# Cross-attention on one Trainium2 core: opening loads on three queues, one context value per slot, and the last values in the score banks

## The chip, the core and the metric

The kernel runs on one core of a Trainium2 chip. The metric is the time of the device in microseconds (us), lower is better. The core has a matrix engine (TensorE, "PE" in the profile, its weight loads "PEld"), three engines for elementwise work (VectorE "DVE", ScalarE "ACT", GpSimd "POOL") and a queue engine that only issues transfers (SyncE, "SP"). ACT and POOL can issue transfers too, from queues of their own. Matrix products are accumulated in PSUM, eight banks of 128 x 512 float32; everything else lies in SBUF, 128 partitions.

## The reference

The input x is 32 batches of 512 rows of 640 columns, the context 32 batches of 77 rows of 1024. The other key and value weights of the signature belong to context rows behind the 77th, which these inputs do not have; only the text part and the outer frame of it count:

```python
q = _heads(hidden_states @ to_q_w)             # 20 heads of 32
k, v = _heads(ehs_txt @ to_k_w), _heads(ehs_txt @ to_v_w)
s = jnp.einsum('bhqd,bhkd->bhqk', q, k) * scale
p = jax.nn.softmax(s, axis=-1)
out = _merge(jnp.einsum('bhqk,bhkd->bhqd', p, v)) @ to_out_w + to_out_b + hidden_states
```

All of it is float32. The kernel keeps this precision by splitting each operand of a large product into a high part (a cast, "hi") and the rest (a subtraction, "lo"), and adding three products: hi x hi, hi x lo, lo x hi.

## The kernel before

The 640 columns are five chunks of 128, each of four heads. A *unit* n is one chunk of one batch, n = 5 b + j; there are 160. The order of the work on every engine and queue is the order in which the program writes it down (a manual schedule); semaphores are put in by the framework. There are four stretches.

*Opening and context, lines 265 to 397.* PE first runs 15 warm-up matmuls on a tile of zeros. The context (2464 rows) is taken in groups of 512 columns, the last of 416, and contracted over eight blocks of 128, k = 0 to 7. For each k three things are loaded, context (cs, line 149), key weights and value weights (wraw, line 99), each as four transfers, one for each quarter of the partitions. VectorE transposes the context (L157), ScalarE casts context and weights (L89), VectorE subtracts (L90), PE forms keys and values (pk and pv, L182). For k = 0 the key products go in three passes: hi x hi for all five chunks, then hi x lo of the context, then lo of the weights. `first` (line 271) writes this down for the first group. Before it stand the first loads: four context quarters on SP, two weight quarters on ACT behind a small copy, two on SP; then POOL waits for the first context quarter (`pause`) and issues the value weights of k = 0 and 1. Keys and values go to DRAM, and are read back per batch (kb and vb). Groups 0 to 3 are done here, and the keys of the last group; its values, five products of 24 matmuls each (`context_values`, chunk by chunk), are left for the next stretch.

*Slots, units 0 to 7, `slot` at line 667.* In slot n PE forms the scores of unit n (L454), the queries of unit n + 1 (L437), and, from slot 3 on, the values of unit n - 3 (L553). VectorE takes maxima (L475), ScalarE takes exponentials (L515) into pn, POOL divides by the sums (L527), VectorE transposes the result into z (`transpose_p`, L534; two buffers, z0 for even units and z1 for odd), and SP moves z into raw with four transfers (`move_p`, L543), which is what PE reads for the values. There are two raw buffers. There is one query buffer (qt0) in this stretch: VectorE copies the queries of unit n + 1 from PSUM into it (L449) before the scores of n + 1. The five values of the last context group are worked in between: chunks 0 and 1 ahead of slot 0, chunk 2 in slot 0, chunks 4 and 3 in slot 1. SP loads the five blocks of output weights (`load_wo`, L665) in slot 1.

PSUM and SBUF change hands in this stretch. Four banks ("sc") hold scores, one ("pq") queries; until the last context value three banks belong to `psv`, after it they become one "po" and two "pa". Where ScalarE has not emptied a score bank in time, `LENT` lets a unit take po or pa for part of its scores. In SBUF the first three value-weight chunks lie in `kva` (wv_s0), the last two with the split context in `kvp` (wv_s1, ct, vs). When these are released the output weights (pool `lw`) take the place of kva, and the pool `late` that of kvp: it holds, in this order, z1 and the two raw buffers, then the rest. In bytes of a partition wv_s0 ends, and wv_s1 begins, at 169952; wv_s1 ends at 186336; z1 takes 168576 to 174720, the first raw buffer 174720 to 182912, the second 182912 to 191104, where ct begins at 186336. The pools are opened with waits per tile: a new tile waits for the last use of those old tiles whose bytes it takes.

*Windows, units 8 to 159, `window` at line 727.* Two units at a time: values, scores of two units, exponentials, one output product (`group`, L602) with its transposition (`turn`, L612) and addition, and queries. Five windows make two batches; the change does not touch them.

*End, `closing` (line 814) and `end` (line 826).* In the last window no queries remain; `closing` puts two output products of the last batch but one in the banks pq and po, turns them, and then takes the values of unit 156 into pq. `end` takes those of 157 into po and the further output products into pq and po again, then the last batch's projection (L634).

Of the kernel before, what the change touches and what calls it, by code (L numbers as in the profile page):

```python
# [37 lines left out]
def kernel(  # L38
# [53 lines left out]
    def load_weights(w, k0, kn, permuted=True, queues=(nc.sync,) * 4, tag="wraw"):  # L92


        raw = kvw.tile([P, 2, C], F32, tag=tag, name="wraw", bufs=3 if tag == "wraw" else 2)
        if permuted:
            rows = w.rearrange("(q c i) n -> q i c n", q=4, i=Q)
            for q, queue in enumerate(queues):
                queue.dma_start(raw[q * Q : (q + 1) * Q, :kn], rows[q, :, k0 : k0 + kn])  # L99
        else:  # L100
            rows = w.rearrange("(c p) n -> p c n", p=P)
            nc.sync.dma_start(raw[:, :kn], rows[:, k0 : k0 + kn])
        for k in range(kn):
            wraws[id(w), k0 + k] = raw[:, k]

    def split_weights(dst, w, k, scale=None, turned=False):

        part = wraws.pop((id(w), k))
        if scale is not None:
            nc.scalar.mul(part, part, scale)  # L110
        hi, lo = dst[:, 0, :], dst[:, 1, :]
        if turned:
            part = part.rearrange("p (q c i) -> p c q i", q=4, i=Q)
            hi, lo = (d.rearrange("p (c q i) -> p c q i", q=4, i=Q) for d in (hi, lo))
        split(hi, lo, part)
# [20 lines left out]
    GROUPS_KV = [(g0, min(G, NT - g0)) for g0 in range(0, NT, G)]  # L136
    cts, pks, pvs, css, craws, wraws = ({} for _ in range(6))

    def load_context(g, *counts):

        g0, gn = GROUPS_KV[g]
        src = ehs_flat[g0 : g0 + gn, :].rearrange("(a j) (q u) -> q j a u", j=Q, q=4)
        if g not in css:
            css[g] = kvc.tile([P, G // Q, NK * Q], F32, tag="cs", name="cs"), [0]
        cs, done = css[g]
        for kn in counts:
            cols = slice(done[0] * Q, (done[0] + kn) * Q)
            for q in range(4):
                nc.sync.dma_start(
                    cs[q * Q : (q + 1) * Q, : gn // Q, cols], src[q, :, :, cols]  # L150
                )
            done[0] += kn
# [9 lines left out]
    def split_context(g, k):  # L162
        gn = GROUPS_KV[g][1]
        ct = kvp.tile([P, 2, G], FPR, tag="ct", name="ct", bufs=9)
        split(ct[:, 0, :gn], ct[:, 1, :gn], craws.pop(k)[:, :gn])
        cts[g, k] = ct
# [57 lines left out]
    def context_values(g, j, pool):  # L224
        values_of(g, j, pool)
        split_values(g, j)
# [44 lines left out]
    def first(*ks):  # L271

        for k in ks:
            transpose_context(0, k)
        for k in ks:
            split_context(0, k)
            split_weights(wk_s[:, k], wk, k)
            for passes in ((0,), (1,), (2,)) if k == 0 else ((0, 1, 2),):
                for j in range(NC_):
                    keys(0, j, k, passes)  # L280
            part = wraws.pop((id(wv), k))
            for (c0, c1), dst in zip(WV, wv_s):
                split(dst[:, k, 0], dst[:, k, 1], part[:, c0:c1])
            for j in range(3):
                values_of_chunk(0, j, k, psk)

    early = kvt.tile([P, P], F32, name="early", bufs=1)
    load_context(0, 1)
    nc.scalar.copy(early[:, :Q], zero[:, :Q].bitcast(F32))
    load_weights(wk, 0, 1, queues=(nc.scalar, nc.scalar, nc.sync, nc.sync))  # L290
    pause = kvt.tile([P, P], F32, name="pause", bufs=1)
    probe = css[0][0][:Q, 0, :Q]
    nc.gpsimd.tensor_tensor(pause[:Q, :Q], probe, probe, ALU.add)
# [237 lines left out]
    def transpose_p(n):  # L531

        pn, z = pnb[n % 2], zs[n % 2]
        nc.vector.transpose(  # L534
            z.rearrange("p c h t j -> p (h t) c j"),
            pn.rearrange("p a (c i) -> p a c i", i=Q),
        )
# [112 lines left out]
        elif h == 1:  # L650
            nc.sync.dma_start(out[last, rows, :], xr)

    LATE, LAG = 2, 3
    EARLY_X = {4: 0, 6: 1}
    LENT = {3: {0: "po", 1: "pa"}, 4: {2: "po", 3: "pa"}, 6: {2: "po", 3: "pa"}}
    held, wos = [], []

    def take(m, tag="pa"):
# [4 lines left out]
    def load_wo(ks):  # L663
        for k in ks:
            nc.sync.dma_start(wos[0][:, k].bitcast(F32), wo_dram[:, k].bitcast(F32))  # L665

    def slot(n, beside=()):
        b, j = divmod(n, NC_)
        copied, last = 3 <= n <= 6, n == FIRST - 1
        views = scores(n)  # L670
        maxima(n, views)
        while held:
            low_a(held.pop())
        if n and not copied and not last:
            transpose_p(n - 1)
        if n == 1:
            load_wo(range(3))
        if j == 0:
            load_keys(b + 1)
        if j == 1:  # L680
            load_values(b)
        if n == 1:
            load_wo(range(3, NC_))
        if n == 0:
            load_x(2)
            load_y(0, range(4))
        for i in range(2):
            exps(n, i)
        if last:
            transpose_p(n - 1)  # L690
        if n >= LATE and not last and not copied:
            move_p(n - 1)
        if len(beside) > 1:
            context_values(LAST, beside[1], psv)
        queries(n + 1, "po" if last else "pq")
        copy_q(n + 1, nc.vector.tensor_copy)
        if copied:
            transpose_p(n - 1)
            move_p(n - 1)
        if n >= LAG and not last:  # L700
            values(n - LAG)
        if last:
            qts.append(late[0].tile([P, S], F32, name="qt1"))
            queries(n + 2)
            copy_q(n + 2, nc.vector.tensor_copy)
        for i in range(2, HPC):
            exps(n, i)
        if not last:
            normalize(n)
        if n == 1:  # L710
            for i in range(NQ):
                transpose_x(2, i)
        if beside:
            context_values(LAST, beside[0], psv)
        if n >= LAG and not last:
            high_a(n - LAG)
            held.append(n - LAG)
        if n in EARLY_X:
            split_x(2, EARLY_X[n])
        if n == 3:  # L720
            load_bias()
        if n < 3:
            split_x(1, n + 2)
# [90 lines left out]
    def closing(n):  # L814

        last = B - 1
        for t in range(NQ):
            load_residual(t)
        for c, tag in ((1, "pq"), (2, "po")):
            group(last - 1, c, range(NC_), tag)  # L820
            turn(last - 1, c)
            add(last - 1, c)
        values(n - 2, "pq")
        high_a(n - 2)

    def end():
# [53 lines left out]
    for c in range(2):  # L880
        split_x(1, c)
    context_values(LAST, 1, psv)
    slot(0, (2,))
    kva.release()
    lw = ctx.enter_context(tc.tile_pool(name="lw", bufs=1, reuse_waits="tile"))
    wos.append(lw.tile([P, NC_, 2, C], FPR, name="wo_s"))
    slot(1, (3, 4))
    psv.release()
    kvp.release()
    late.append(ctx.enter_context(tc.tile_pool(name="late", bufs=1, reuse_waits="tile")))  # L890
# [2 lines left out]
    )  # L893
    zs.append(late[0].tile(ZSHAPE, F32, name="z1"))
    move_p(0)
    for n in range(LATE, FIRST):
        slot(n)
    for n in range(FIRST, N, 2):
# [42 lines left out]
```

## Time and profile before

| what | us |
|---|---|
| median of 3 runs | 1691.91 (1691.86 to 1692.5) |
| profiled execution, its own time | 1692.86 |
| its span, first to last instruction | 1690.8 |
| TensorE busy | 1683.6 |
| ScalarE busy | 1075.9 |
| VectorE busy | 1010.5 |
| GpSimd busy | 990.1 |

The profile is that of one execution. In a timeline a row gives start, duration, engine, line and operation, "out<-in" by tile names, shapes, a count where rows are merged, and in brackets how long the engine had been idle and what released it. "SPq", "ACTq" and "POOLq" are transfers being issued, not moving. In the table by engine a row is a stretch: its length, then the busy time of PE, PEld, DVE, ACT and POOL with the number of instructions, then the granted TensorE clock, the DMA engines' busy share and GB/s. The chain of waits follows back from the last instruction what released each step. A row of transfers gives count, size and the median time from issue to landing.

### The profile page before, as it was taken

The page shows a single profiled execution, that of the slowest core. Times are in us where ns is not written, and L with a number is a line of the kernel's source. Part 1 is how long each engine was busy: PE and PEld are TensorE (multiplying, and loading weights), DVE is VectorE, ACT ScalarE, POOL GpSimd, SP SyncE. Part 2 cuts the span into 40 slices and gives each one's busy share as a digit, 9 for nine tenths or more (in the row PEclk, how much of TensorE's full clock was granted, in tenths as well). Part 3 has the DMA queues.
Part 4 walks back from the last instruction along what each step waited for, and adds up shares of the span by engine and source line. Part 5 has one row for each costly group of instructions (what it writes and reads, how often), then busy time and mean ns, then how long its engine had stood idle before and what let it go on. Part 6 is the DMA issues. An engine that isn't in the chain of part 4 may idle for free.

```text
span 1690.8 us, 36827 instructions
## 1 busy us (share of the span) xinstructions
PE 1683.6 (100%) x12460; PEld 1303.9 (77%) x12460; DVE 1010.5 (60%) x1635; ACT 1075.9 (64%) x5622; POOL 990.1 (59%) x663
## 2 busy tenths in 40 slices
PE   9999999999999999999999999999999999999999
PEld 7888898777777777777777777777777777777777
DVE  4341235766676666766666657576666766667653
ACT  3231125867677676776767767677676776767762
POOL 1000026667667666667575766767667676766755
PEclk9999999999999999999999999999999999999999
DMA  9847558678889787879797988888979788888956
GB/s 182 159 94 189 121 103 229 150 173 188 190 187 204 172 204 175 202 181 212 166 211 166 211 181 195 185 194 186 203 173 204 173 202 190 188 192 183 210 136 187
DMA packets 363852, 306.51 MB, mean 181 GB/s; under 512 B 88784, under 2 KB 292112, under 8 KB 363664
## 3 DMA queue, kind: packets, MB, share of 16 engines
q1 hardware_dynamic: 360864, 296.61, 78.4%
q0 software_dynamic: 2704, 7.38, 1.4%
q8 instruction: 99, 1.62, 0.4%
q14 instruction: 89, 0.73, 0.1%
q10 hardware_dynamic: 96, 0.16, 0.0%
HBM read 120.36 MB, written 57.88 MB: 105 GB/s over the span
## 4 chain that ended last, share of the span: by engine, by line
PE 97%; DMA 1%; ACT 0%; DVE 0%; SPq 0%; issue 0%; POOL 0%; DVEq 0%; ACTq 0%
PE pq L437 32%; PE po L602 31%; PE pv L182 7%; PE pk L182 7%; PE sc L454 6%; PE po L553 4%; PE pq L553 4%; PE pa L454 3%; DMA wraw<-in_L_xattn_to_k_w_dram 1%; PE sc L634 1%; PE pa L553 0%; ACT pn L515 0%; DMA cs<-in_ctx_dram 0%; PE pa L634 0%; PE pq L602 0%; SPq L99 0%
## 5 line engine op out<-in xcount | busy, mean ns | idle before, releaser
L515 ACT ACTIVATE pn<-sc,nm 128x77 f32<-128x77 f32 x1928 | 597.3, 367 | 131.4 <-DVE nm L508 102.8
L437 PE MATMUL pq<-xt,wq_s 128*128 128x512 f32 x2349 | 559.0, 390 | 0.0
L602 PE MATMUL po<-at,wo_s 128*128 128x512 f32 x2295 | 554.6, 393 | 0.0
L437 PEld LDWEIGHTS pq<-xt,wq_s 128*128 128x128 f32 x2349 | 440.6, 188 | 91.4
L602 PEld LDWEIGHTS po<-at,wo_s 128*128 128x128 f32 x2295 | 425.1, 188 | 90.8
L515 ACT ACTIVATION_READ_ACCUMULATOR pn<-sc,nm 128x1 f32 x1928 | 477.3, 249 | 0.0
L527 POOL TENSOR_TENSOR pn<-pn,rs 128x1232 f32<-128x1232 f32 x160 | 363.6, 2273 | 125.3 <-DVE rs L525 121.8
L616 POOL TENSOR_TENSOR xs<-xs,ot 128x512 f32<-128x512 f32 x155 | 199.8, 1289 | 322.1 <-DVE ot L612 314.4
L534 DVE STREAM_TRANSPOSE z<-pn 128x1536 f32<-128x1536 f32 x160 | 282.3, 1765 | 113.7 <-POOL pn L527 92.2
L259 POOL TENSOR_TENSOR xt<-xs,xt 128x512 fp32r<-128x512 f32 x157 | 198.5, 1293 | 35.8 <-ACT xt L258 35.8
L515 ACT ACTIVATE pn<-pa,nm 128x77 f32<-128x77 f32 x620 | 200.5, 382 | 0.0
L587 POOL TENSOR_TENSOR xs<-xs,bias_y 128x640 f32<-128x640 f32 x124 | 192.4, 1574 | 0.2
L567 ACT CAST at<-po 128x512 fp32r<-128x512 f32 x77 | 45.1, 585 | 230.1 <-PE po L553 230.1
L508 DVE TENSOR_REDUCE nm<-sc 128x6 f32<-128x462 f32 x304 | 177.1, 624 | 15.2 <-PE pa L454 15.2
L449 DVE COPY qt<-pq 128x512 f32<-128x512 f32 x83 | 57.4, 691 | 210.1 <-PE pq L437 210.1
L454 PE MATMUL sc<-kb,qt 32*128 32x77 f32 x3856 | 161.9, 273 | 0.0
L515 ACT ACTIVATION_READ_ACCUMULATOR pn<-pa,nm 128x1 f32 x620 | 161.0, 263 | 0.0
L454 PEld LDWEIGHTS sc<-kb,qt 32*128 32x128 f32 x3856 | 149.4, 187 | 4.2 <-issue 2.2
L182 PE MATMUL pk<-ct,wk_s 128*128 128x512 f32 (+1 forms) x600 | 134.0, 382 | 0.7 <-ACT wk_s L89 0.5
L182 PE MATMUL pv<-ct,wv_s 128*128 128x512 f32 (+1 forms) x600 | 134.2, 382 | 0.0
L454 PEld LDWEIGHTS pa<-kb,qt 32*128 32x128 f32 x1240 | 83.9, 186 | 63.7 <-ACT at L567 63.7
L182 PEld LDWEIGHTS pk<-ct,wk_s 128*128 128x128 f32 x600 | 112.1, 188 | 20.9 <-ACT wk_s L89 1.2
(81 smaller groups left out, 1339.7 us busy)
## 6 DMA issues: line engine op xcount, KB each, us to landing
raw<-z SPq DMA_DIRECT2D x640, 192.0 KB, 3.4
xs<-in_x_dram SPq DMA_DIRECT2D x256, 320.0 KB, 6.3
out_dram<-xs SPq DMA_DIRECT2D x127, 320.0 KB, 4.8
vb<-v_dram SPq DMA_DIRECT2D x32, 240.0 KB, 4.4
kb<-k_dram SPq DMA_DIRECT2D x32, 192.5 KB, 4.6
cs<-in_ctx_dram SPq DMA_DIRECT2D x12, 512.0 KB, 9.0
k_dram<-ks POOLq DMA_DIRECT2D x20, 256.0 KB, 2.5
v_dram<-vs SPq DMA_DIRECT2D x80, 64.0 KB, 2.4
```

The source lines that it names most:

```text
L182: nc.tensor.matmul(held[j][:, :gn], w[:, k, a, :], cts[g, k][:, c, :gn], start=(k == 0 and n == 0), stop=(k == NK - 1 and n == 2),)
L259: low.tensor_tensor(parts[1], src, parts[0].bitcast(F32), ALU.subtract)
L437: nc.tensor.matmul(pqs[n], wq_s[:, k, a, j * P : (j + 1) * P], xts[b, k][:, c, :], start=(k == 0 and m == 0), stop=(k == NC_ - 1 and m == 2),)
L454: nc.tensor.matmul(out, qt_of(n)[r, t * P : (t + 1) * P], kbs[b % 2][r, j, :], start=True, stop=True, tile_position=(i * HD, 0),)
L508: nc.vector.tensor_reduce(nm, view, AX.X, ALU.max, negate=True)
L515: nc.scalar.activation(pnb[n % 2][:, at, :NKEY], scs.pop((n, i, t)), AF.Exp, bias=nms.pop((n, i, t)), accum_out=sms[n][:, at : at + 1],)
L527: nc.gpsimd.tensor_tensor(pf, pf, rs.unsqueeze(2).to_broadcast([P, NQ * HPC, NKEY]), ALU.mult)
L534: nc.vector.transpose(z.rearrange("p c h t j -> p (h t) c j"), pn.rearrange("p a (c i) -> p a c i", i=Q),)
L553: nc.tensor.matmul(pas[n][i * HD : (i + 1) * HD, :].rearrange("p (a q) -> p a q", q=P), vb[:, i, :], raw[:, :, i, :], start=True, stop=Tru ...
L587: nc.gpsimd.tensor_tensor(part, part, biases[1].unsqueeze(1).to_broadcast([P, 4, U]), ALU.add)
L602: nc.tensor.matmul(pos[b, c], wos[0][:, k, a, c * P : (c + 1) * P], ats[b * NC_ + k][:, d, :], start=(k == 0 and m == 0), stop=(k == NC_ - ...
L616: nc.gpsimd.tensor_tensor(part, part, ots.pop((b, c)).rearrange("p (a i) -> p a i", i=Q), ALU.add)
```

## The change

Three parts. In the opening the fourth context quarter of k = 0 goes from SP to ACT, ahead of the small copy there, and the fourth quarter of the first key weights from SP to POOL, ahead of its wait; the high part of the first key weights is cast by VectorE ahead of the context's subtraction, and no longer by ScalarE. In the slots the last three context values are one in each of slots 0, 1 and 2, chunks 3, 4 and 2, always behind the queries; the pools change hands behind slot 2 and no longer within slots 0 and 1; probabilities of units 0 and 1 are moved there (that of unit 1 is transposed there too); the output weights are loaded in slots 3 (three blocks) and 4 (two); slot 3 lends no banks. At the end the values of unit 156 (`values(n - 2)` with n = 158) are put in a "pa" bank.

```diff
@@ -136,7 +136,7 @@
     GROUPS_KV = [(g0, min(G, NT - g0)) for g0 in range(0, NT, G)]
     cts, pks, pvs, css, craws, wraws = ({} for _ in range(6))
 
-    def load_context(g, *counts):
+    def load_context(g, *counts, queues=(nc.sync,) * 4):
 
         g0, gn = GROUPS_KV[g]
         src = ehs_flat[g0 : g0 + gn, :].rearrange("(a j) (q u) -> q j a u", j=Q, q=4)
@@ -146,7 +146,7 @@
         for kn in counts:
             cols = slice(done[0] * Q, (done[0] + kn) * Q)
             for q in range(4):
-                nc.sync.dma_start(
+                queues[q].dma_start(
                     cs[q * Q : (q + 1) * Q, : gn // Q, cols], src[q, :, :, cols]
                 )
             done[0] += kn
@@ -273,8 +273,15 @@
         for k in ks:
             transpose_context(0, k)
         for k in ks:
-            split_context(0, k)
-            split_weights(wk_s[:, k], wk, k)
+            if k == 0:
+                part = wraws.pop((id(wk), k))
+                hi, lo = wk_s[:, k, 0, :], wk_s[:, k, 1, :]
+                nc.vector.tensor_copy(hi, part)
+                split_context(0, k)
+                nc.vector.tensor_tensor(lo, part, hi.bitcast(F32), ALU.subtract)
+            else:
+                split_context(0, k)
+                split_weights(wk_s[:, k], wk, k)
             for passes in ((0,), (1,), (2,)) if k == 0 else ((0, 1, 2),):
                 for j in range(NC_):
                     keys(0, j, k, passes)
@@ -285,9 +292,9 @@
                 values_of_chunk(0, j, k, psk)
 
     early = kvt.tile([P, P], F32, name="early", bufs=1)
-    load_context(0, 1)
+    load_context(0, 1, queues=(nc.sync, nc.sync, nc.sync, nc.scalar))
     nc.scalar.copy(early[:, :Q], zero[:, :Q].bitcast(F32))
-    load_weights(wk, 0, 1, queues=(nc.scalar, nc.scalar, nc.sync, nc.sync))
+    load_weights(wk, 0, 1, queues=(nc.scalar, nc.scalar, nc.sync, nc.gpsimd))
     pause = kvt.tile([P, P], F32, name="pause", bufs=1)
     probe = css[0][0][:Q, 0, :Q]
     nc.gpsimd.tensor_tensor(pause[:Q, :Q], probe, probe, ALU.add)
@@ -650,9 +657,10 @@
         elif h == 1:
             nc.sync.dma_start(out[last, rows, :], xr)
 
-    LATE, LAG = 2, 3
+    LATE, LAG = 3, 3
+    WO = {3: range(3), 4: range(3, NC_)}
     EARLY_X = {4: 0, 6: 1}
-    LENT = {3: {0: "po", 1: "pa"}, 4: {2: "po", 3: "pa"}, 6: {2: "po", 3: "pa"}}
+    LENT = {4: {2: "po", 3: "pa"}, 6: {2: "po", 3: "pa"}}
     held, wos = [], []
 
     def take(m, tag="pa"):
@@ -671,16 +679,12 @@
         maxima(n, views)
         while held:
             low_a(held.pop())
-        if n and not copied and not last:
-            transpose_p(n - 1)
         if n == 1:
-            load_wo(range(3))
+            transpose_p(0)
         if j == 0:
             load_keys(b + 1)
         if j == 1:
             load_values(b)
-        if n == 1:
-            load_wo(range(3, NC_))
         if n == 0:
             load_x(2)
             load_y(0, range(4))
@@ -688,15 +692,13 @@
             exps(n, i)
         if last:
             transpose_p(n - 1)
-        if n >= LATE and not last and not copied:
-            move_p(n - 1)
-        if len(beside) > 1:
-            context_values(LAST, beside[1], psv)
         queries(n + 1, "po" if last else "pq")
         copy_q(n + 1, nc.vector.tensor_copy)
         if copied:
             transpose_p(n - 1)
             move_p(n - 1)
+        if n in WO:
+            load_wo(WO[n])
         if n >= LAG and not last:
             values(n - LAG)
         if last:
@@ -710,8 +712,8 @@
         if n == 1:
             for i in range(NQ):
                 transpose_x(2, i)
-        if beside:
-            context_values(LAST, beside[0], psv)
+        for c in beside:
+            context_values(LAST, c, psv)
         if n >= LAG and not last:
             high_a(n - LAG)
             held.append(n - LAG)
@@ -820,7 +822,7 @@
             group(last - 1, c, range(NC_), tag)
             turn(last - 1, c)
             add(last - 1, c)
-        values(n - 2, "pq")
+        values(n - 2)
         high_a(n - 2)
 
     def end():
@@ -880,11 +882,11 @@
     for c in range(2):
         split_x(1, c)
     context_values(LAST, 1, psv)
-    slot(0, (2,))
+    for n, c in enumerate((3, 4, 2)):
+        slot(n, (c,))
     kva.release()
     lw = ctx.enter_context(tc.tile_pool(name="lw", bufs=1, reuse_waits="tile"))
     wos.append(lw.tile([P, NC_, 2, C], FPR, name="wo_s"))
-    slot(1, (3, 4))
     psv.release()
     kvp.release()
     late.append(ctx.enter_context(tc.tile_pool(name="late", bufs=1, reuse_waits="tile")))
@@ -893,6 +895,8 @@
     )
     zs.append(late[0].tile(ZSHAPE, F32, name="z1"))
     move_p(0)
+    transpose_p(1)
+    move_p(1)
     for n in range(LATE, FIRST):
         slot(n)
     for n in range(FIRST, N, 2):
```

## The prediction

> **What bounds the kernel now.** I read the page first: its busy shares and the chain that ended last.
>
> ```profile
> span 1690.8 us, 36827 instructions
> PE 1683.6 (100%) x12460; PEld 1303.9 (77%) x12460; DVE 1010.5 (60%) x1635; ACT 1075.9 (64%) x5622; POOL 990.1 (59%) x663
> PE 97%; DMA 1%; ACT 0%; DVE 0%; SPq 0%; issue 0%; POOL 0%; DVEq 0%; ACTq 0%
> ```
>
> TensorE (PE) is the bound. It idles 1690.8 - 1683.6 = 7.2 us, part of it before the first matmul and after the last one, which the change leaves. It removes no matmul, so it can only win back pauses of PE, or make new ones. I therefore looked up each pause in the list of waits of PE and in the timeline; there are three places, and the change touches each of them.
>
> First the opening, in the timeline, the chain between 21 and 35 us, and the stretches from 2 us.
>
> ```profile
> 1.46 6.39 PE L269 MATMUL warm<-zero 128*128 128x512 f32 x15 [1.46 <-DVE zero L266]
> 6.28 0.71 DVE L157 STREAM_TRANSPOSE craw<-cs 128x512 f32<-128x512 f32 x1 [4.87 <-DMA cs<-in_ctx_dram]
> 7.02 0.62 ACT L89 CAST ct<-craw 128x512 fp32r<-128x512 f32 x1 [4.77 <-DVE craw L157]
> 7.55 0.72 ACT L89 CAST wk_s<-wraw 128x640 fp32r<-128x640 f32 x1
> 8.30 0.82 DVE L90 TENSOR_TENSOR wk_s<-wraw,wk_s 128x640 fp32r<-128x640 f32 x1
> 8.32 3.70 PE L182 MATMUL pk<-ct,wk_s 128*128 128x512 f32 x15 [0.47 <-ACT wk_s L89]
> ...
> 21.95 7.82 DMA wraw<-in_L_xattn_to_k_w_dram
> 31.51 3.25 PE pk L182 x13
> ...
> 2.00:2.50 0.50, 0.50 (x3) 0.35 (x2) 0.00 (x0) 0.24 (x2) 0.00 (x0) 1.00 0.93 146
> 2.50:3.00 0.50, 0.50 (x3) 0.40 (x2) 0.00 (x0) 0.00 (x0) 0.00 (x0) 1.00 0.33 53
> 3.00:3.50 0.50, 0.50 (x3) 0.40 (x2) 0.00 (x0) 0.00 (x0) 0.33 (x2) 1.00 0.61 171
> 3.50:4.00 0.50, 0.50 (x3) 0.40 (x2) 0.00 (x0) 0.00 (x0) 0.50 (x1) 1.00 0.84 188
> ```
>
> The warm-up matmuls end at 7.85; the first key matmul starts at 8.32, when ScalarE, which casts the context first, has cast the weights. But the chain does not pass through that point. It passes through the key weights of chunk 4, which land at 29.77, and reaches PE at 31.51: the opening is bound by the stream of loads. In the last four rows the second number from the right is the DMA share: from 2 to 4 us it is below 1.
>
> **Part 1, the opening.** The eight first loads now leave from SP (three context quarters, one weight quarter), ACT (one context, two weight quarters) and POOL (one weight quarter). SP's next loads start two issues earlier, about 1 us at the half microsecond that one takes (six in these two rows: 1.98 + 0.95 = 2.93).
>
> ```profile
> 0.75 1.98 SPq L149 DMA_DIRECT2D cs<-in_ctx_dram  x4
> 2.77 0.95 SPq L99 DMA_DIRECT2D wraw<-in_L_xattn_to_k_w_dram  x2
> ```
>
> What the stream can win is what the DMA engines idled while loads waited to be issued: 0.5 x (0.07 + 0.67 + 0.39 + 0.16) = 0.65 us. The bounds are 0 (the k = 4 weights land no earlier) and 1.0 (both saved issues). I take 0.6. The cast of the first key weights goes from ScalarE (0.72) to VectorE (0.83 at most, the subtraction of the same shape), beside ScalarE's context cast instead of behind it. PE can then start when the warm-up is over, 0.47 earlier; behind it the two subtractions on VectorE start up to 0.83 later, but their products are the second and third passes, 5 and 10 matmuls of 3.70/15 = 0.25 us later, so 1.2 and 2.5 us cover them. This 0.47 is no second gain: it is spent waiting at k = 4 unless the stream is earlier too. POOL's quarter is issued ahead of its wait for the first context; the eight value loads behind it do not move, and ACT's first load costs it nothing that is waited for. Opening: -0.6.
>
> **Part 2, the slots.** The timeline around slots 2 and 3 (PE, VectorE, SP), then two stretches of the table by engine.
>
> ```profile
> 286.23 3.68 PE L437 MATMUL pq<-xt,wq_s 128*128 128x512 f32 x15
> 289.94 0.69 DVE L449 COPY qt<-pq 128x512 f32<-128x512 f32 x1 [0.31 <-PE pq L437]
> 290.69 0.33 PE L454 MATMUL po<-kb,qt 32*128 32x77 f32 x1 [0.78 <-DVE qt L449]
> 295.40 1.07 PE L553 MATMUL pa<-raw,vb 96*32 96x512 f32 x8
> 292.10 0.42 DVE L475 TENSOR_REDUCE nm<-po 128x4 f32<-128x308 f32 x1
> 296.11 1.77 DVE L534 STREAM_TRANSPOSE z<-pn 128x1536 f32<-128x1536 f32 x1
> 286.59 2.98 SPq L543 DMA_DIRECT2D raw<-z  x2
> ...
> 271.50:285.20 13.70, 13.70 (x100) 12.71 (x99) 8.28 (x13) 5.52 (x33) 8.95 (x11) 1.00 0.80 288
> 290.70:322.40 31.70, 31.70 (x291) 22.24 (x294) 23.52 (x41) 29.53 (x175) 17.08 (x12) 1.00 0.62 153
> ```
>
> Slot 2 now ends with a context value, 4.5 us of matmuls between its queries and the scores of slot 3. The copy of the query (0.69) hides under it, and the wait of 0.78 goes: -0.8. The sum of PE's work in the three slots is the same, so slot 3 starts near 289.8.
>
> What comes later in exchange: (a) the second transposition into z1 waits until the last context value is done, because z1's bytes overlap the first value weights, which that value reads; it then runs ahead of slot 3's maxima on VectorE, and ends near 289.8 + 0.62 (its value transposed) + 1.77 = 292.2. The maxima start there, as they do today at 292.10. So ScalarE's exponentials of slots 3 to 7 do not get earlier, and ScalarE is busy 29.53 of 31.7 us there. PE's lead of 0.8 runs into banks that ScalarE frees; I give back 0.3. (b) The first move of transposed probabilities needs the first raw buffer. By the sizes of the tiles, in the order in which the pools stack them, it lies within the value weights of chunks 3 and 4, and these are read last in slot 1, by 280.6. SP has nothing else in slot 2, so it moves at once, and values 0 (PE near 294.6) does not wait. The second move starts near 292.2; issues take 2.6 us and the landing 3.5 (rows below), so it lands near 298.3, before values 1 at 301.08 - 0.8 = 300.3. (c) Five output weights (640 KB each) move from slot 1 to slots 3 and 4, on SP's queue ahead of the moves for values 3 and 4. Today they run beside the first stretch above, at a share of 0.80: 0.80 x 13.7 = 11 us with a value load and value stores. From 290.7 to 322.4 the share is 0.62, which leaves 0.38 x 31.7 = 12 us. They fit, barely. The moves of slot 2 land near 302.4; three weights at 288/0.80 = 360 GB/s take 5.5 us, the third move of four 192 KB 2.2 us: 310.1. Values 3 needs it at 312.44 - 0.8 = 311.6. I charge 0.2 for delays.
>
> ```profile
> 309.31 2.56 SPq L543 DMA_DIRECT2D raw<-z  x4
> 312.44 1.07 PE L553 MATMUL pa<-raw,vb 96*32 96x512 f32 x8
> raw<-z SPq DMA_DIRECT2D x4, 192.0 KB, 3.5
> raw<-z SPq DMA_DIRECT2D x2, 192.0 KB, 5.0
> vb<-v_dram SPq DMA_DIRECT2D x1, 240.0 KB, 7.3
> vb<-v_dram SPq DMA_DIRECT2D x32, 240.0 KB, 4.4
> ```
>
> The two raw rows are the second move (from 289.6) and the last pair of the first (from 286.59). The last two rows price (c) in another way: the value load behind three output weights landed after 7.3 us (stretch 273 to 273.5), against 4.4 in the median of all.
>
> [...]
>
> Slots: -0.8 + 0.3 + 0.2 = -0.3. Bounds: -0.8, and the two slower rivals below.
>
> **Part 3, the end.**
>
> ```profile
> 1644.48 0.86 PE pq L553 x8
> 1658.16 1.07 PE L553 MATMUL pq<-raw,vb 96*32 96x512 f32 x8 [0.45 <-DVE ot L612]
> 1659.53 1.07 PE L553 MATMUL po<-raw,vb 96*32 96x512 f32 x8 [0.30 <-DMA raw<-z]
> 1659.91 0.69 DVE L572 TENSOR_TENSOR at<-pq,at 128x512 fp32r<-128x512 f32 x1 [1.21 <-ACT at L567]
> 1660.66 3.71 PE L602 MATMUL pq<-at,wo_s 128*128 128x512 f32 x15
> ```
>
> Values N-4 leave the query bank for a score bank, which ScalarE has emptied by then, so their wait of 0.45 for the transposition of that bank goes. But values N-3 behind them wait for a DMA that lands at 1659.3 whatever PE does. What remains is that the next output group no longer waits for the subtraction that ends at 1660.60 to free the query bank; it can follow values N-3, whose eight matmuls occupy PE for 0.86 (the first row, the same step a window earlier in the chain): 1659.53 + 0.86 = 1660.39 instead of 1660.66. End: -0.3 (bounds 0 and -0.75, both waits).
>
> **Sum.** -0.6 - 0.3 - 0.3 = -1.2 us. The profiled execution took 1692.86 us (span 1690.8 and 2.06 around it); so it would be 1691.7. It lies 0.95 above the median of the runs, 1691.91; on the median the forecast is 1690.7.
>
> **Rivals.**
> - *Weights block the moves (slower).* If the five weights run at the rate per share of slots 3 to 7, 153/0.62 = 247 GB/s, three take 8.0 and a move 3.2 us: 302.4 + 11.2 = 313.6, and values 3 wait 2.0 us; the other two (5.3), a key load and two more moves (0.8 + 6.4) end at 326.1, 2.5 us behind values 5 even so. That is +4.5 in place of 0.2: 1690.7 + 4.3 = 1695.0. It decides once the weights are slower than about 300 GB/s. For it: the order of the queue. Against it: the rate of 360 today.
> - *The first move waits for slot 2's context value.* If the first raw buffer is freed only with the last context value, the move starts at 289.8 instead of 280.6. Today its second pair is issued from 286.59 to 289.57, beside the value stores, and lands 5.0 after its issues, so near 293.3; 4.5 later is 297.8, and values 0, due at 295.40 - 0.8 = 294.6, wait 3.2 us: 1693.9. Against it: the sizes above, and that SP waits per tile.
> - *Nothing is won.* The loads land no earlier, since 128-byte pieces fill the engines anyway, and ScalarE takes back the whole 0.8: 1690.7 + 0.6 + 0.5 = 1691.8, no change. For it: ScalarE's 29.53 of 31.7.
> - *All pauses go*: -1.0 - 0.8 - 0.75 = -2.6, 1689.3. That is the floor; it needs every bound at once.
>
> **How the numbers follow.** Two tenths of a per cent, 3.4 us, is about what a measurement can tell from no change here. Chances: the forecast 0.53 (its own range 1689.9 to 1691.4), nothing won 0.16, first move waits 0.12, weights block 0.15, floor and others 0.04. The range 1689.8 to 1694.2 takes in the first three and the milder half of the fourth. Faster by over 0.2% would need more than the floor: 0.03. Slower by over 0.2% needs 1695.3: the harder half of the weights' case, or it together with the first move: 0.11. Same: 0.86.
>
> **What would show it.** Opening: DMA share near 1 from 2.5 us on, the first key matmul by 7.9, the k = 4 weights landing near 29.2. Slots: no wait for the query copy near 290; the first raw moves issued near 281, no wait of PE for raw in slots 3 to 8; if PE waits for raw at values 0, the second rival holds, at values 3 or 5 the first. End: no wait for the transposed bank, but a wait of about 0.7 for raw. The forecast is wrong if PE shows a wait over 2 us anywhere, or if the time from the start of the first window to the end changes by more than 1 us.

## The result, and the profile after

The changed kernel takes 1696.83 us (median of 8, 1694.02 to 1697.63) against 1692.1 (median of 8, 1691.83 to 1692.59) for the kernel before, run in turn with it: a ratio of 1.0027, 95% interval 1.0017 to 1.0036. It is slower by 4.7 us. The forecast was 1690.7 with a range up to 1694.2, and no measurable change was held the likeliest; it was wrong. A second measurement, e5 below, gave 1695.54 (11 runs), ratio 1.0021 (1.0012 to 1.003).

The page of the changed kernel's profiled execution (1695.34 us) and then its list of waits of TensorE (us in total, times, longest):

```profile
span 1693.1 us, 36822 instructions
PE 1684.4 (99%) x12460; PEld 1303.7 (77%) x12460; DVE 1011.3 (60%) x1636; ACT 1077.6 (64%) x5621; POOL 991.6 (59%) x664
PE 96%; DMA 2%; SPq 1%; DVE 0%; issue 0%; ACT 0%; DVEq 0%; ACTq 0%
```

```profile
PE pa L560 <- DMA raw<-z: 2.3, 1, 2.3
PE warm L269 <- DVE zero L266: 1.5, 1, 1.5
PE pk L182 <- ACT ct L89: 0.7, 1, 0.7
PE po L560 <- DVE ot L619: 0.5, 1, 0.5
```

TensorE has the same 12460 matmuls but is busy 0.8 us longer, and one new wait of 2.3 us heads its list: values that wait for a move of probabilities, the thing which the prediction said must not appear. The wait of 0.8 for the query copy is gone. The timeline shows where the wait stands.

```profile
261.79 1.13 PE L461 MATMUL sc<-kb,qt 32*128 32x77 f32 x32
280.29 18.87 SPq L550 DMA_DIRECT2D raw<-z  x12
289.38 1.13 PE L461 MATMUL sc<-kb,qt 32*128 32x77 f32 x32
294.06 1.06 PE L560 MATMUL pa<-raw,vb 96*32 96x512 f32 x8
299.47 1.93 SPq L673 DMA_DIRECT2D wo_s<-wo_dram  x3
302.29 2.71 SPq L550 DMA_DIRECT2D raw<-z  x4
305.04 1.49 SPq L673 DMA_DIRECT2D wo_s<-wo_dram  x2
313.55 1.78 DVE L541 STREAM_TRANSPOSE z<-pn 128x1536 f32<-128x1536 f32 x1 [1.57 <-DMA raw<-z]
313.56 1.06 PE L560 MATMUL pa<-raw,vb 96*32 96x512 f32 x8 [2.31 <-DMA raw<-z]
315.92 2.90 PE L444 MATMUL po<-xt,wq_s 128*128 128x512 f32 x6
320.79 1.78 DVE L541 STREAM_TRANSPOSE z<-pn 128x1536 f32<-128x1536 f32 x1 [2.57 <-DMA raw<-z]
```

SP issues three output weights at 299.47, then the four pieces of the move for the values of unit 3, then two more weights. Values 3 (313.56) have waited 2.31 us for that move, where before they began at 312.44 without a wait. VectorE waits for this move too before its next transposition into z, and for the move of unit 4 before the one after it, since z is still being read. Two TensorE rows after the wait six query matmuls take 2.90 us, which take 1.65 where the clock is full (1.66 at the same place in the timeline of before).

The chain of waits names the transfer, and the table of transfers issued between 303 and 305 us gives its time from issue to landing (count, size, median us):

```profile
304.27 9.15 DMA raw<-z
...
raw<-z SPq DMA_DIRECT2D x3, 192.0 KB, 9.1
```

A move took 3.5 us in the prediction's rows. The table by engine shows how full the DMA engines were, first after and then before, over the same stretches (the last three columns are the granted clock, the DMA engines' share, and GB/s):

```profile
300.00:311.00 11.00, 11.00 (x110) 7.68 (x102) 9.00 (x16) 10.76 (x64) 7.13 (x7) 1.00 1.01 291
311.00:315.20 4.20, 1.89 (x34) 0.83 (x32) 2.61 (x3) 4.15 (x26) 0.60 (x1) 1.00 1.02 335
315.20:318.70 3.50, 3.50 (x27) 2.78 (x21) 2.50 (x7) 2.73 (x16) 3.09 (x2) 0.51 1.09 272
```

```profile
300.00:311.00 11.00, 11.00 (x111) 7.44 (x110) 8.70 (x16) 10.76 (x64) 7.13 (x8) 1.00 0.69 163
311.00:315.20 4.20, 4.20 (x50) 2.69 (x49) 3.19 (x5) 4.20 (x29) 1.08 (x1) 1.00 0.89 229
```

From 300 us on the DMA engines are full (1.01, 1.02, 1.09; a packet is counted whole in the stretch in which it starts, so a share can exceed 1) where they stood at 0.69 and 0.89. What stands ahead of the move in its queue shows in the landings of the single transfers of this trace. The last piece of the move for the values of unit 2 lands at 302.05, the three weights at 304.94, 308.05 and 310.29, the four pieces of the late move at 310.99, 311.75, 312.61 and 313.43, and only then the other two weights, at 314.77 and 316.63: what SP issued lands in the order in which it was issued. In the second stretch TensorE works 1.89 of 4.20 us; in the third its clock is halved (0.51).

Where the 2.34 us between the two spans (1693.13 and 1690.79) come from, by the starts of the same steps in the two timelines:

| stretch on TensorE | before | after | difference |
|---|---|---|---|
| start to scores of unit 0 | 262.28 | 261.79 | -0.49 |
| scores of unit 0 to scores of unit 3 | 28.41 | 27.59 | -0.82 |
| scores of unit 3 to values of unit 3 | 21.75 | 24.18 | +2.43 |
| values of unit 3 to values of unit 4 | 9.08 | 10.68 | +1.60 |
| values of unit 4 to values of unit 154 | 1321.89 | 1321.89 | 0.00 |
| values of unit 154 to the end | 47.38 | 47.00 | -0.38 |

The loss lies whole between the scores of unit 3 and the values of unit 4. The halved clock is enough for the +1.60: 3.41 us at half speed (below) do the work of 1.7. In e2, at full clock, another wait costs 0.86 us in the same stretch.

These two executions lie closer together than the medians: the one of before took 1692.86 us, 0.8 above its median, and the one of the changed kernel 1695.34, 1.5 below its own. The table explains 2.3 us, not 4.7. Among the eight runs of the changed kernel the single one with a granted clock of 1.000 is the quickest (1694.02), and the three with 0.998 took 1697.24 to 1697.53.

### The profile page after: what moved, and what is told of

Same layout as the page of the kernel before. It is cut to its first block, busy times and chain, and to the rows that moved or that the text cites. A ratio compares the mean times of both kernels' runs of the same rounds, so it can differ in the third digit from the quotient of the medians.

```text
span 1693.1 us, 36822 instructions
## 1 busy us (share of the span) xinstructions
PE 1684.4 (99%) x12460; PEld 1303.7 (77%) x12460; DVE 1011.3 (60%) x1636; ACT 1077.6 (64%) x5621; POOL 991.6 (59%) x664
## 4 chain that ended last, share of the span: by engine, by line
PE 96%; DMA 2%; SPq 1%; DVE 0%; issue 0%; ACT 0%; DVEq 0%; ACTq 0%
PE pq L444 32%; PE po L609 31%; PE pv L182 7%; PE pk L182 7%; PE sc L461 6%; PE po L560 5%; PE pq L560 4%; PE pa L461 3%; DMA wraw<-in_L_xattn_to_k_w_dram 1%; DMA raw<-z 1%; PE sc L641 1%; PE po L444 0%; SPq L550 0%; SPq L99 0%; PE pa L641 0%
```

## The experiments

The theory after the first comparison: the output weights, moved to slots 3 and 4, stand ahead of the moves and delay them (the prediction's rival "weights block the moves"); the wait leaves TensorE partly idle, and its clock is then halved for a while, as in the profile above (0.51; the expectations say that the gate closes). The rival: part 2 loses time for another reason (the opening, the order of the context values, the banks that slot 3 no longer borrows). Parts are undone or done alone. In each timed group the kernel before was run beside; its median was 1692.32 in the first (e1 to e4), 1692.27 in the second (e5 to e8) and 1692.12 in the third (e9 to e12).

**e1: the changed kernel, one output weight in each of slots 3 to 7.**

```diff
-    WO = {3: range(3), 4: range(3, NC_)}
+    WO = {n: (n - 3,) for n in range(3, FIRST)}
```

> The changed kernel, with the five output weights loaded one per slot in slots 3 to 7 instead of three in slot 3 and two in slot 4. Queue theory (three and two weights ahead of the moves on SP's ring make TensorE wait 2.3 us at the values of unit 3, and that idle stretch closes the TensorE clock gate): no wait of TensorE for raw over 0.5 us in slots 3 to 8, clock 1.000, and the sum of the three gains, 0.5 + 0.8 + 0.4 us: a median near 1690.4. Rival (the late first moves and transpositions, not the weights, make the wait): still a wait near 2 us at the values of unit 3, and 1694 to 1697.

1692.52 us, ratio 1.0002 (0.9994 to 1.0011); the loss is gone. The timeline of its trace, and the table of the transfers issued between 302 and 306 us:

```profile
311.89 1.06 PE L560 MATMUL pa<-raw,vb 96*32 96x512 f32 x8
322.45 1.06 PE L560 MATMUL pq<-raw,vb 96*32 96x512 f32 x8 [0.37 <-DMA raw<-z]
...
raw<-z SPq DMA_DIRECT2D x4, 192.0 KB, 3.6
```

With one weight ahead of it instead of three, the same move lands in 3.6 us instead of 9.1, and values 3 do not wait. Nothing else of part 2 was undone, so the loss is that of the weights' place. The fullness of the engines alone does not make the wait, as the table by engine of e1 shows:

```profile
300.00:305.00 5.00, 5.00 (x54) 3.36 (x53) 3.98 (x8) 5.00 (x31) 3.53 (x6) 1.00 0.97 274
305.00:310.00 5.00, 5.00 (x53) 3.34 (x52) 3.79 (x7) 4.90 (x31) 2.60 (x3) 1.00 0.96 264
```

In the changed kernel the share in these two stretches is 1.00 and 0.99, hardly more. What differs is what lands ahead of the move: one weight at 306.15, then the four pieces from 306.90 to 308.64. The forecast gain of e1 (1690.4) did not come, though: 0.37 us remain as a wait at the values of unit 5, and the time is that of the kernel before.

**e2: the changed kernel, with ten extra matmuls ahead of the values of unit 3.** Their result is overwritten by the values; they only keep TensorE at work while it would wait.

```diff
     def values(n, tag="pa", fill=0):
...
+        for _ in range(fill):
+            nc.tensor.matmul(pas[n], wq_s[:, 0, 0, :P], xts[1, 0][:, 0, :], start=True, stop=True)
...
-            values(n - LAG)
+            values(n - LAG, fill=10 if n == 6 else 0)
```

> The changed kernel, with ten matmuls (0.23 us each) whose result is overwritten put in front of the values of unit 3, so that TensorE works through the stretch in which it waited 2.3 us. Gate theory: the wait itself stays (the values still start when raw lands), but the clock stays granted, 1.000 in every run; a median near 1694.0, the fastest run of the changed kernel, and a spread under 1 us. Rival (the spread of 1694.0 to 1697.6 comes from transfers that take longer in some runs): median and spread stay, near 1696.8 and 3 us.

1695.35 us, ratio 1.0019 (1.001 to 1.0028). The granted clock was 1.000 in all 11 runs, against 1.000 in one of the changed kernel's eight. In the timeline the extra matmuls fill the wait, and the move comes still later than they end:

```profile
312.26 2.51 PE L560 MATMUL pa<-xt,wq_s 128*128 128x512 f32 x10 [0.16 <-DVE at L581]
315.55 1.06 PE L562 MATMUL pa<-raw,vb 96*32 96x512 f32 x8 [0.77 <-DMA raw<-z]
325.49 1.07 PE L562 MATMUL po<-raw,vb 96*32 96x512 f32 x8 [0.78 <-DVE qt L456]
```

So the halved clock follows from the idle time, and it is not the main loss: with a full clock throughout the kernel is still 3.0 us slower than before. (Its extra 2.5 us take the place of the wait, and 0.77 are added; the wait of 0.78 behind it is VectorE, which is late with the query copy because its transposition waited for the next move, that of unit 4.) The time expected was 1694.0 with a spread under 1 us; it came out 1.4 higher, with a spread of 2.4. What makes that spread with the clock at 1.000 stays open.

**e3: part 2 alone on the kernel before** (opening and end as before), and **e4: only the weights moved on the kernel before** (order of the context values, pools and banks as before). The edit of e4, shortened:

```diff
-        if n == 1:
-            load_wo(range(3))
...
-        if n == 1:
-            load_wo(range(3, NC_))
...
+        if n in (3, 4):
+            load_wo(range(3) if n == 3 else range(3, NC_))
```

> The kernel before with the second part of the change alone (slots and output weights; opening and end as before). Queue theory: the whole loss is in this part, so the time is the changed kernel's plus the two small gains of the other parts (0.5 + 0.4): a median near 1697.5 with a spread of 2 to 4 us, and a TensorE wait near 2.3 us at the values of unit 3. Rival (the opening or the end costs something that the slots win back): below 1695.

> The kernel before with the output weights alone moved, three to slot 3 and two to slot 4, as in the change; context values, pools and moves as before. Queue theory: TensorE comes to the values of unit 3 about 0.8 us later than in the changed kernel, so it waits 1 to 2 us there; whether the clock gate closes on that is open: 1693.3 to 1696. Rival (it takes the rearranged slots): no wait over 0.5 us, 1692.1.

e3: 1697.8 us, ratio 1.0031 (1.0019 to 1.0043). e4: 1696.93 us, ratio 1.0029 (1.0018 to 1.004). The move of the weights alone, with nothing else of the change, costs as much as the whole change, and more than expected (1693.3 to 1696). The list of waits of e3, and its stretch from 326 to 330 us:

```profile
PE pa L553 <- DMA raw<-z: 2.1, 1, 2.1
PE po L553 <- DVE qt L449: 1.9, 1, 1.9
```

```profile
326.00:330.00 4.00, 4.00 (x68) 3.51 (x64) 1.83 (x4) 2.30 (x5) 3.76 (x3) 0.51 0.78 182
```

Here a second wait, VectorE's, is nearly as large as the first, and the clock is halved behind it; it comes back after 6.83 us. e4 shows the same two waits, of 2.80 and 1.93 us, and it too is halved behind the second alone. Both traces are of the longest run of their group (1699.24 and 1699.94 us, 1.4 and 3.0 above the medians), so the second wait need not be there in every run.

**e5: the changed kernel again.**

> The changed kernel once more, beside the next three on the same chip. Gate theory: in each run the time over the runs with clock 1.000 is the time lost at half rate, half of what the clock is below 1 (3.4 us a window, 1.7 us of loss); medians near 1696.8, most runs with a clock of 0.999 or 0.998. Rival (the clock is a bystander): times and clocks unrelated.

1695.54 us, ratio 1.0021 (expected near 1696.8). The 3.4 us of the expectation is how long the halved clock lasts in the profile after (3413 ns from 315.24 us). The eleven runs fall in two kinds: six with a granted clock of 1.000, 1694.59 to 1695.54 us (median 1695.15), and five below it, 1696.22 to 1697.44. So the waits alone cost 1695.15 - 1692.27 = 2.9 us, and the halved clock 1.1 to 2.3 us more where it comes. The profiled run is one of the five:

```profile
313.80:320.70 6.90, 6.90 (x49) 4.66 (x42) 3.87 (x7) 5.05 (x28) 3.50 (x2) 0.51 1.07 294
```

It was expected that a run loses half of the time at half clock. For these 6.8 us that is 3.4, and this run lies 2.0 above the median of those with a full clock. A halved stretch may hide waits that would stand there otherwise; this was not tested.

**e6: the changed kernel, its first output weight ahead of the second move (before slot 3), one each in slots 3 to 6.**

```diff
-    WO = {3: range(3), 4: range(3, NC_)}
+    WO = {n: (n - 2,) for n in range(3, 7)}
...
     move_p(0)
+    load_wo((0,))
     transpose_p(1)
     move_p(1)
```

> The changed kernel with one output weight in front of the second move (behind slot 2) and one each in slots 3 to 6, so that none is left in slot 7. Queue theory: the wait of 0.4 us at the values of unit 5 that the one-per-slot kernel had is gone, no wait for raw over 0.2 us, clock 1.000: 1.2 to 1.6 us below the kernel before. Rival (the transfers of slots 3 to 7 together are too many, whatever their order): a wait moves to the values of unit 1 or 3 and the time stays at that of the kernel before.

1692.94 us, ratio 1.0008 (0.9998 to 1.0018). Values 3 do not wait, but the values of unit 5 start at 322.67, 1.14 us after those of unit 4 (320.46 + 1.07) have ended. The last piece of their move lands at 322.48. The 1.2 to 1.6 us that the theory expected to win did not come: an earlier start of the weights does not remove the last wait, and from 311 to 319 us the engines are full here too (0.98 and 1.06). One of the eleven runs took 1701.64 us at a clock of 0.996; why is not known.

**e7: parts 1 and 3 alone on the kernel before; e8: the kernel before, run once more beside it.**

> The kernel before with the first and the third part of the change, without the second (slots). Theory: both gains are real and add up, 0.5 + 0.4: 0.9 us below the kernel before, clock 1.000, no spread beyond that of the kernel before. Rival (the opening's gain is lost in the slots or was only a gate that opened earlier): within 0.4 us of the kernel before.

> The kernel before, unchanged, for its trace on this chip: 1692, waits of TensorE as in its first profile (0.5 at the first key matmul, 0.8 before the scores of unit 3, 0.4 and 0.3 at the end), clock 1.000.

e7: 1692.34 us, ratio 1.0001 (0.9993 to 1.001); the 0.9 that the prediction gave to the two parts is not there. e8: 1692.68, span 1690.6. So the parts were taken one by one.

**e9: part 1 alone. e10: part 3 alone.**

> The kernel before with part 1 alone (opening loads on three queues, VectorE casts the first key weights). The forecast's step says -0.6 us, so a ratio near 0.9996 and the keys' end of the opening 0.6 us earlier. The theory now, from the positions of the scores of unit 0 in six traces (261.8 us on average with either opening, scatter about 1 us): 0 within +-0.3, ratio 1.0000, the first key matmul about 0.5 earlier (7.4 to 7.7 instead of 7.9 to 8.3) and this given back where the loads of later chunks bind.

> The kernel before with part 3 alone (values of unit 156 in a score bank). The forecast's step says -0.3 us. The theory now agrees: the stretch from the values of unit 154 to the end takes 47.0 to 47.1 us instead of 47.4, and the ratio is 0.9998; the rival says that the values of unit 157 wait as long for their transfer as the whole gain, so 47.4 and 1.0000.

e9: 1692.77 us, ratio 1.0005 (0.9996 to 1.0014). e10: 1692.09 us, ratio 0.9999 (0.999 to 1.0009). Neither wins. In e9 the first key matmul starts at 7.51, but the scores of unit 0 at 262.09; in e10, whose opening is that of before, they start at 260.82. At the end, after first and then e10:

```profile
1660.37 1.07 PE L560 MATMUL pa<-raw,vb 96*32 96x512 f32 x8
1661.96 1.06 PE L560 MATMUL po<-raw,vb 96*32 96x512 f32 x8 [0.53 <-DVE ot L619]
```

```profile
1658.22 1.06 PE L553 MATMUL po<-raw,vb 96*32 96x512 f32 x8 [0.96 <-DMA raw<-z]
```

The values of unit 156 wait for nothing now. Those of unit 157, one step on, wait for what comes last, a bank in one trace and the move in the other. In e10 the stretch from the values of unit 154 to the end is 47.38 us, none of the gain left. The 0.65 us by which e9 is slower than the kernel before lie within its interval.

**e11: the changed kernel, its five weights issued by POOL instead of SP. e12: the same, with one weight in each of slots 3 to 7.**

```diff
-            nc.sync.dma_start(wos[0][:, k].bitcast(F32), wo_dram[:, k].bitcast(F32))
+            nc.gpsimd.dma_start(wos[0][:, k].bitcast(F32), wo_dram[:, k].bitcast(F32))
```

> The changed kernel, its five output weights still loaded in slots 3 and 4, but issued by POOL instead of SP, so that no move stands behind a weight in SP's queue. If the order in SP's queue makes the wait at the values of unit 3 (theory), the move shares the engines with the weights and lands before 312.5: no wait there over 0.3 us, 1691.5 to 1693 us, ratio 0.9995 to 1.0005. If it is the sum of the bytes that the engines carry between 300 and 313 us, or the slow 2 KB pieces of the moves themselves (rival), the wait of about 2 us stays, 1694.5 to 1696.5, ratio near 1.002. A small wait may appear at the values of unit 4 or 5, since the five weights are then spread over the same time.

> The changed kernel with one output weight in each of slots 3 to 7, issued by POOL. Both theories expect no wait at the values of unit 3. If the order of the queue made the 0.37 us at the values of unit 5 with the same spread on SP, it goes: the slots' -0.8 and the end's -0.35 are all left, 1691.0 to 1691.8 and a ratio near 0.9994. If the engines are too full for any wait to go, 1692.0 to 1692.8 and a ratio near 1.0001.

e11: 1697.77 us, ratio 1.0035 (1.0022 to 1.0047); e12: 1693.41 us, ratio 1.0012 (1.0003 to 1.0022). Each lies above both of the ranges expected for it. My theory that the order in SP's queue alone makes the wait fell: away from that queue the weights do more harm. The timeline, the chain and a stretch of e11, then the transfers issued between 294.4 and 299 us:

```profile
294.48 1.67 POOL L673 DMA_DIRECT2D wo_s<-wo_dram  x3
298.89 11.37 DMA raw<-z
310.39 1.94 PE L560 MATMUL pa<-raw,vb 96*32 96x512 f32 x8 [4.67 <-DMA raw<-z]
304.00:310.00 6.00, 1.73 (x8) 1.11 (x6) 2.28 (x5) 5.13 (x33) 3.15 (x2) 0.89 1.06 254
...
raw<-z SPq DMA_DIRECT2D x5, 192.0 KB, 10.5
```

POOL issues three weights at 294.48, 5 us earlier than SP did. The move for the values of unit 2, in a queue with no weight ahead of it, then takes 11.37 us from its last issue, and those values wait 4.67. A wait thus needs no order of a queue; the engines are full (1.06 from 304 to 310 us), and they serve both queues. (The trace is of e11's longest run, 1700.78 us, 3.0 above the median of its five.) From 294.4 to 299 us POOL's queue had 48.7% of the engines' time and SP's 43.1%, so a queue of its own gave the move a share of the engines, and no precedence. That the 2 KB pieces of the moves are slow, as the rival has it, shows in the changed kernel's trace from 304 to 313.5 us, where at the median a packet of 2048 bytes took 131.5 ns and one of 5120 bytes, as the weights have them, 200; what this makes of the wait was not separated. In e12 the wait at values 3 is gone, but one of 2.83 stands at the values of unit 5:

```profile
315.97 8.62 DMA raw<-z
324.72 1.07 PE L560 MATMUL pq<-raw,vb 96*32 96x512 f32 x8 [2.83 <-DMA raw<-z]
```

That trace is of a run of 1698.91 us, 5.5 above the median of e12, so a wait of 2.83 is not the usual one. By the medians SP (e1, 1.0002) does better than POOL (e12, 1.0012) with the same spread, but their intervals overlap. A reason would be that in SP's queue a weight waits behind the moves that were issued ahead of it, while in POOL's it takes its share beside them; this is argued and not shown. e11 changes two things at once, the queue and the time at which the weights start; how much of its 4.67 us each makes was not separated.

## Why the prediction was wrong

*Part 2 (c) is the step that failed.* It let three weights and one move pass in 5.5 + 2.2 = 7.7 us from 302.4 and charged 0.2. The last piece of the move landed at 304.27 + 9.15 = 313.42, 11.0 us after 302.4 instead of 7.7, and the term of 0.2 measured 2.4 up to the values of unit 3; the whole change costs 2.9 in the runs with a full clock (e5), what the slots gain already taken off. By the landings in the changed kernel's trace, the three weights took 8.2 us from 302.05 to 310.29 where the prediction has 5.5, and the move 3.1 behind them where it has 2.2. Three things were wrong in it:

- The rate. 360 GB/s was read off a stretch in which the weights moved beside little else. Three weights and four pieces of 192 KB are 2688 KB; in 11.0 us that is 250 GB/s. The engines carried about 300 in that time (291 and 335 in the table after), the difference going to the other transfers that were due. The rival's 247 was the right number: its 8.0 and 3.2 us stand against 8.2 and 3.1, and its 313.6 lies 0.2 from the landing seen.
- The idle share. That 38% of the engines' time was free from 290.7 to 322.4 was true and did not help. The move landed behind all that SP had issued ahead of it (its pieces from 310.99 us on, the third weight at 310.29); that the engines had idle time elsewhere in the 31.7 us did not bring it forward. e1 loads the same bytes over five slots, its engines are nearly as full from 300 to 310 us (0.97, 0.96), and its ratio is 1.0002.
- The follow-up. In the sum values 3 were the only waiter. VectorE also waits for the moves, before it may overwrite z; its query copies stand behind that transposition, and TensorE waited for them up to 1.9 us (e3, e4).

*Not in the prediction at all: the clock.* After the wait the granted clock is 0.51, in the profiled run from 315.24 to 318.65 us, 3413 ns by the trace's clock records; in e5 and e3 6827, in e11 10240 ns, so once, twice and three times the same length. The time before the fall was not idle throughout: TensorE worked 1.89 of 4.20 us in it. And work alone did not end the halved clock at once: in e5 it lasted two such lengths although TensorE was busy throughout (6.90 of 6.90 us). With matmuls in the gap the clock stayed at 1.000 in all 11 runs (e2). What sets the length of a halved stretch, and when it ends, is not shown.

*The rival "weights block the moves" was right in its place and mechanism.* Its first wait, 2.0 us at values 3, measured 2.31, 2.12 (e5) and 2.13 (e3). Its second, 2.5 at values 5, is in no trace of the changed kernel; in e3 VectorE's wait of 1.9 at values 4 stands in its place. That its 1695.0 lies so near the 1695.15 of e5's runs with a full clock is therefore half luck. It was given 0.15. What should have raised it stood in the prediction: the value load behind three weights took 7.3 us instead of 4.4, a delay of 2.9 for whatever stands behind three weights, and the slack of the third move was only 311.6 - 310.1 = 1.5. Its reason, the order of SP's queue, holds for the changed kernel, whose landings follow that order; it is not the only way to such a wait, for in e11 no weight stands ahead of the move in its queue, and the wait is longer.

*The other steps of part 2.* The query copy's wait went, -0.82 by the table where -0.8 was forecast; the 0.3 that ScalarE was to take back was not seen: in e1, where the moves hardly wait, the stretch from the scores of unit 3 to the values of unit 3 takes 21.97 us, before 21.75, so 0.2 at most up to there. The first move started at 280.29, as worked out from the sizes of the tiles (280.6), and values 0 did not wait; "the first move waits for slot 2's context value" is ruled out.

*Part 1, -0.6, fell.* Its markers came true in the profile of the changed kernel. The timeline, the chain, and the stretches from 2 us:

```profile
7.36 2.83 PE L182 MATMUL pk<-ct,wk_s 128*128 128x512 f32 x11 [0.72 <-ACT ct L89]
21.33 7.93 DMA wraw<-in_L_xattn_to_k_w_dram
2.50:3.00 0.50, 0.50 (x3) 0.40 (x2) 0.00 (x0) 0.21 (x1) 0.00 (x0) 1.00 1.45 235
3.00:3.50 0.50, 0.50 (x3) 0.40 (x2) 0.00 (x0) 0.00 (x0) 0.00 (x0) 1.00 0.88 135
```

The shares of 0.33 and 0.61 became 1.45 and 0.88, the first key matmul starts at 7.36 (by 7.9 was said), the k = 4 weights land at 29.26 (29.2 was said). Yet the same landing moves by as much with the opening unchanged: 29.25 in e3, 29.77 before; in the nine traces with the new opening it lies between 29.26 and 30.08. The start of the scores of unit 0 is 262.28, 262.07, 261.82, 261.35 and 260.82 in the five traces with the old opening (mean 261.7), and between 261.79 and 262.65 in the nine with the new one (mean 262.1). The step took one trace's opening for the kernel's, and its scatter, 1.5 us, is larger than the term. That small pieces fill the engines, the reason of the rival "nothing is won", is in the trace of before from 2.2 to 2.7 us: 586 packets, 570 of them of 128 bytes, had 93.9% of the engines' time at 146 GB/s. What sets the length of the opening behind k = 4 stays open.

*Part 3, -0.3, is not shown.* The stretch from the values of unit 154 to the end is 47.4 to 47.5 us in the five traces with the old end, and 46.76 to 47.41 in the seven with the new one whose weights SP loads (mean 47.1, so -0.3; with POOL's weights, e11 and e12, it is 48.0 and 48.2). But e10 alone shows no gain in its time. The reason is the one which the step named: the values of unit 157 wait for what comes last.

The sum -0.6 - 0.3 - 0.3 became, in the profiled run, -0.49 (scatter) - 0.82 + 2.43 + 1.60 - 0.38 = +2.34. With the weights spread over the slots on SP (e1) the remaining parts bring the kernel level with the one before, and no version measured here beats both.

## What to carry to other kernels

A transfer that is moved onto the path of small urgent ones must be weighed against the slack of each of those, in its own 5 or 10 us: the mean idle share over 30 us (38%) did not show the wait here (2.31 us), and the rate was that of the mixed traffic (250 GB/s), not the one read off the weights when they ran beside little else (360). Spreading such loads one by one in the same queue, behind the urgent transfers, took the loss away (e1, ratio 1.0002); a second queue did not protect these here (e11, 1.0035), since it shared the engines (48.7% of their time, against 43.1% for SP's). A term below the scatter of its stretch between executions (here 1.5 us in the opening) can't be taken from one trace: look at the same stretch in several before it enters a sum.

## What the runs showed of the hardware

- TensorE's clock was halved after a stretch in which it still worked 45% (1.89 of 4.20 us), for 3413, 6827 or 10240 ns, and not in every run of the same kernel: six of eleven in e5 kept 1.000. The same wait thus costs 1.1 to 2.3 us more or less.
- Longer waits did not always halve it: in e4 one of 2.80 us left it full and one of 1.93 behind it halved it, in e3 one of 2.13 left it full and one of 1.9 behind it halved it. In the 3413 ns before each fall (as long as the halved stretch of the changed kernel) TensorE idled 1.74 us in the changed kernel, 2.12 in e5, 1.81 in e3 and 1.88 in e4. A limit can't be read off these traces; they show only that 3.4 us about half idle can stand before a halved clock, and that a wait as long need not bring one.
- Transfers of 192 KB that land in 3.5 us among others like them took 9.1 behind three 640 KB weights of the same queue, and 10.5 beside three weights of another queue. Within SP's queue they landed in the order of issue, at engine shares that hardly differ (1.00 with three weights ahead, 0.97 with one).
- The first warm-up matmuls, the same in all kernels, take 5.18 us in the changed kernel's trace, 6.39 in that of before, and 5.36 in a second trace of before (e8): the traces' clock records have the full clock from 4.62, 7.28 and 5.04 us on, so how soon it is granted changes from run to run.
